# Relative-position attention: a doubled row written by ScalarE, one block copied by GpSimd, and values copied one unit later

## The chip, the cores and the metric

The kernel runs on one NeuronCore of a Trainium2 chip. The metric is the device time of one execution, in microseconds. Engines are named as in the profile: PE (TensorE, with its weight loads as PEld), DVE (VectorE), ACT (ScalarE), POOL (GpSimd) and SP (SyncE, which here issues the DMAs; its queue is SPq).

## The reference

Four layers are applied to x of 4 sequences with 1024 positions and 128 features, in float32: `x = x + attn(LN(x)) * silu(ffn(LN(x)))`, each layer with its own attn and ffn. Layers 0 to 2 (a state-space layer, an entmax attention, a recurrent layer, and their ffns) are not touched. The last layer, cut to what matters here:

```
q, k, v = split_head(x @ Wq.T), split_head(x @ Wk.T), split_head(x @ Wv.T)   # 16 heads of 8
ex = rel_embed[arange(1024) + (256 - 1024)] per head     # a table of 256 rows
srel = srel_skew(einsum('bhnd,hmd->bhnm', q, ex))        # pad by one column, reshape, cut
qk = (einsum('bhnd,bhmd->bhnm', q, k) + srel) / sqrt(8)
out = softmax(qk - 1e9 * upper_triangle) @ v  @ Wp.T + bp
ffn = down(silu(gate(x)) * up(x))                        # int8 weights, scaled by 1/127
```

So a score has a second part, the product of a query with the embedding of its distance to the key. `srel_skew` pads the products with distances by a zero column and reads them with a row length one shorter: row r of the skewed matrix begins one element further than row r - 1. The table has 256 rows and the index runs from -768 to 255: the last 256 distances take rows 0 to 255, the 256 before them the same rows again (negative indices count from the end), and all further ones row 0. The kernel subtracts row 0 from the table, which softmax does not see, so that a tile of queries needs products only for the key tiles 0 to 4 back: the block 3 back equals the block 1 back, the blocks 2 and 4 back are made from the products of the block 0 back by masks.

## The kernel before

`tile_kernel` loads the constants, runs layers 0 to 2, and then `layer3`. A tile framework gives out buffers of rotating pools, inserts the semaphores, and sets the order of instructions on each engine from the order of the program with some reordering; SP, ACT, POOL and DVE then work through their queues in that order.

In `layer3` four heads lie together in one group (partitions 32j to 32j + 8 hold head j), there are 16 groups (4 batches x 4), and each group has 8 query tiles of 128 positions, taken in the order ORDER3 = 7, 0, 6, 1, 5, 2, 4, 3. That makes 128 units n. A unit goes through these steps:

- `relative3` (called by `part`, seven half-pairs ahead): for two heads and two query tiles, PE multiplies q with the embeddings of the distances (L1914) into two PSUM tiles `pr` of the tag "tr", which has 3 buffers and which `ffn3`, `begin3`, `finish3` and `end3` use too. ACT copies each to SBUF `r` (L1916, a pool of 3 buffers). SP stores r to a DRAM tile `flat` of rows with 384 columns, the last 128 of which repeat the first 128 (four DMAs, L1919 and L1920).
- `shear3` (called by `ahead`, three units ahead): SP reads `flat` back to `rel` with a row step of 383 instead of 384, which does the skew. L1935 reads the blocks 1 and 0 back, L1937 the block of tile t = 0, L1941 the block 3 back where t is at least 3. POOL then makes the blocks 2 and 4 back and the causal mask with `affine_select` (L1945). Tile rel has two buffers for t > 3 and one for the others.
- `scores3`: PE multiplies q and k (L1978) into the only score buffer, four PSUM banks for four heads. DVE scales them, adds rel, and keeps the minimum of the negated scores (L1986 for columns without rel, L1993 with it). ACT takes the exponential and the sums (L2000).
- One tile later DVE transposes the weights (L1737), and PE multiplies them with the values (`weigh3`, L2014). The values lie in one tile `vb`, spread out by four POOL copies of `vr` (`values3`, L1899) when the last weighing of a group is through.
- `project3` loads the next group's q and k, with a POOL memset of q's first column (L1881). `finish3` (L2025 to L2035) divides by the sums, `end3` (L2041 to L2055) projects, and `begin3` and `ffn3` (L1855 to L1872: ACT's silu and copy of up, POOL's product h, PE's po) do the layer norm, q, k, v of the next batch and the ffn beside the units of chosen groups. L228 is a helper that updates x, on POOL.

Of the kernel before, what the change touches and what calls it, by code (L numbers as in the profile page):

```python
# [19 lines left out]
P = 128  # L20
# [9 lines left out]
def _constants():  # L30
    i = np.arange(P)
    row, col = i[:, None], i[None, :]
    parts = []

    def rows(a):
        a = np.asarray(a, np.float32)
        return np.ascontiguousarray(np.broadcast_to(a.reshape(1, -1), (P, a.size)))

    parts.append(("ident", np.eye(P)))
    parts.append(("tri", row <= col))  # L40
    parts.append(("neg_ssd", np.where(col >= row, 0.0, -1e30)))
    parts.append(("tril", col < row))
    parts.append(("bd8", np.kron(np.eye(16), np.ones((8, 8)))))
    parts.append(("bd16", np.kron(np.eye(8), np.full((16, 16), 1.0 / 16.0))))
    parts.append(("ones", np.ones((P, P))))

    parts.append(("sel3", (row // 32 == col // 8 % 4) & (row // 8 % 4 == col // 32)))
    parts.append(("of_a", (row // 8 % 4) == np.arange(4)[None, :]))
    parts.append(("of_t", (row % 8) == np.arange(8)[None, :]))
# [43 lines left out]
class Kit:  # L93


    def __init__(self, tc, const, const_sb):
        self.tc, self.nc = tc, tc.nc
        self.const_sb = const_sb
        self.n_copy = 0
        self.ident = self.c("ident")  # L100
        self.ident16 = const.tile([P, P], BF16, tag="ident16", name="ident16")
        self.nc.vector.tensor_copy(self.ident16, self.ident)
        self.pick = const.tile([24, 8, P], BF16, tag="pick", name="pick")

    def c(self, name):
        at, n = CONST_AT[name]
        return self.const_sb[:, at : at + n]

    def copy(self, out, in_):

# [1561 lines left out]
def layer3(k, W, x3, out, eps5, ps):  # L1672
# [12 lines left out]
    with ExitStack() as st:  # L1685
# [7 lines left out]
        def part(h):  # L1693

            at, h = divmod(h, 8)
            if at < 4 * NB:
                pair = ORDER3[h // 4 * 4 + h // 2 % 2] // 2
                if h % 2 == 0:
                    flats[at, pair] = dram.tile([2, 4, P, 384], F32, tag="flat", name="flat")
                relative3(k, W, temp, ps, flats[at, pair], group[at]["q"], at % 4, pair, h % 2)  # L1700

        def ahead(n):
# [5 lines left out]
            for n, (b, i, t) in enumerate(units):  # L1708
                yield from scores3(k, p1, p2, ps, group[n // 8], rels.pop(n), t)

        batch[0] = {}
        drain(begin3(k, W, p1, p2, temp, ps, dram, x3, 0, eps5, batch[0]))
        group[0] = {}
        drain(project3(k, p2, batch[0], 0, group[0]))
# [6 lines left out]
        weights, transposes, weighs, out_of = {}, [], [], {}  # L1721

        def transpose(n, heads):

# [14 lines left out]
                weighs.append((big, weigh(n)))  # L1739

        def weigh(n):
            nonlocal values
            b, i, t = units[n]
            at, pair = n // 8, t // 2
            if n % 8 == 2:
                out_of[at] = ps.tile([P, 8, 32], F32, tag="o", name="po")
            o = out_of[at]
            yield from weigh3(k, weights.pop((at, pair)), vb, o, pair)
            if n % 8 == 7:
                drain(values)  # L1750
                if i == 0:
                    batch[b]["on"] = p1.tile([P, 4, 256], F32, tag="on", name="on")
                finish3(k, p1, ps, o, group[at]["sums"], batch[b]["on"][:, i, :])
                if i == 3:
                    end3(k, W, temp, ps, x3, b, batch[b], out[b])
            yield
# [12 lines left out]
        for x, (n, first) in enumerate(tiles + [(len(units), 0)] * 4):  # L1769
            next(fill, None)  # L1770
            if transposes and transposes[0][0] < x:
                transpose(*transposes.pop(0)[1:])
            step()
            next(fill, None)
            last = n < len(units) and (x + 1 == len(tiles) or tiles[x + 1][0] > n)
            if not last:
                continue
            b, i, t = units[n]
            at, pos = n // 8, n % 8
            transposes += [(x, n, heads) for heads in (((0, 1), (2, 3)) if t > 3 else ((0, 1, 2, 3),))]  # L1780
            if pos == 0 and at + 1 < 4 * NB:
                group[at + 1] = {}
                project = project3(k, p2, batch[(at + 1) // 4], (at + 1) % 4, group[at + 1])
            if pos == 0 and i == 1:
                beside = ffn3(k, W, p1, temp, ps, batch[b])
            if pos == 3 and i == 2 and b + 1 < NB:
                batch[b + 1] = {}
                beside = begin3(k, W, p1, p2, temp, ps, dram, x3, b + 1, eps5, batch[b + 1])
            if pos == 0:

                next(project, None)
            part(n + 7)
            if pos == 2:
                next(project, None)
            if pos == 6 and at + 1 < 4 * NB:
                values = values3(k, p1, batch[(at + 1) // 4], vb, (at + 1) % 4)
                next(values)
            next(beside, None)
            ahead(n + 3)
        while weighs:  # L1800
            step()

# [73 lines left out]
def project3(k, p2, seq, i, group):  # L1876

    nc = k.nc
    q = p2.tile([P, 1 + T], F32, tag="q", name="q")
    kk = p2.tile([P, T], F32, tag="k", name="k")  # L1880
    nc.gpsimd.memset(q[:, 0:1], 0.0)  # L1881
# [20 lines left out]
def relative3(k, W, temp, ps, flat, q, i, pair, jp):  # L1902
# [2 lines left out]


    nc = k.nc
    r = temp.tile([P, 2, 2, 256], F32, tag="temp", name="r")
    js = (2 * jp, 2 * jp + 1)
    pr = [ps.tile([P, 2, 256], F32, tag="tr", name="pr") for _ in js]  # L1910
    for m in range(2):
# [1 line left out]
            at, t = slice(32 * j, 32 * j + 8), 2 * pair + m  # L1913
            nc.tensor.matmul(to[:, m, :], q[at, t * P : (t + 1) * P], W["emb"][at, i, :], start=True, stop=True)  # L1914
    for n, to in enumerate(pr):
        nc.scalar.copy(r[:, n], to)  # L1916
    rows = flat.rearrange("m j p u -> p j m u")
    for m in range(2):
        nc.sync.dma_start(out=rows[:, 2 * jp : 2 * jp + 2, m, 0:256], in_=r[:, :, m])  # L1919
        nc.sync.dma_start(out=rows[:, 2 * jp : 2 * jp + 2, m, 256:384], in_=r[:, :, m, 0:P])  # L1920


def shear3(k, pool, flat, t):
# [6 lines left out]
    rel = pool.tile([P, 4, min(t, 4) + 1, P], F32, tag="relb" if t > 3 else f"rels", name="rel")  # L1930
    slot = lambda back: min(t, 4) - back

    shear = lambda n: bass.AP(base.tensor, base.offset + t % 2 * 4 * P * 384 + P, [(383, P), (P * 384, 4), (1, n)])
    if t:
        nc.sync.dma_start(out=rel[:, :, slot(1) : slot(1) + 2, :].rearrange("p n s c -> p n (s c)"), in_=shear(256))  # L1935
    else:
        nc.sync.dma_start(  # L1937
            out=rel[:, :, 0, :], in_=bass.AP(base.tensor, base.offset + 2 * P, [(383, P), (P * 384, 4), (1, P)])
        )
    if t >= 3:  # L1940
        nc.sync.dma_start(out=rel[:, :, slot(3), :], in_=shear(P))  # L1941

    def select(back, sign, op, fill):

# [129 lines left out]
def tile_kernel(ctx: ExitStack, tc: tile.TileContext, I, out):  # L2074

    nc = tc.nc
    const = ctx.enter_context(tc.tile_pool(name="const", bufs=1))
    n_const = CONST_AT["pick"][0]
    const_sb = const.tile([P, n_const], F32, tag="const_sb", name="const_sb")
    nc.sync.dma_start(out=const_sb, in_=I["const"][:, 0:n_const])  # L2080
    k = Kit(tc, const, const_sb)
    eps5 = const.tile([P, 1], F32, tag="eps5", name="eps5")
    nc.vector.memset(eps5, 1e-5)
    store = ctx.enter_context(tc.tile_pool(name="x3", bufs=1, space=DRAM))
    x3 = store.tile([P, NB * NT, D], F32, tag="x3", name="x3")
    whole = ExitStack()
    xp = whole.enter_context(tc.tile_pool(name="x", bufs=1, side="right"))
    x_all = xp.tile([P, NB * NT, D], F32, tag="x_all", name="x_all")

    right = ExitStack()  # L2090
# [54 lines left out]
```

## Time and profile before

| | |
|---|---|
| median of 3 runs | 3262.25 us (3260.37 to 3266.85) |
| the profiled execution | 3261.59 us, of which its span is 3259.9 us |
| mean granted TensorE clock | 0.734 |
| PE busy over the span | 2317.2 us (71%) |
| DVE busy | 2307.1 us (71%) |
| ACT busy | 1487.5 us (46%) |
| POOL busy | 1174.5 us (36%) |
| `layer3` | about 2182 to 3260 us of the span |

Busy time of an engine is the time of its instructions without its waiting; its share is an average over four very different layers, so that the stretch of `layer3` has to be read by itself. In a list of waits, a row names the engine, its tile and line, what released it, and then the idle microseconds, how many times, and the longest. A row of groups gives busy time and mean nanoseconds of one, then the idle time just before its instructions with what ended it.

### The profile page before, as it was taken

How to read it: one execution, taken by the hardware profiler on the slowest of the kernel's cores; microseconds unless marked ns; L12 is line 12 of the kernel's file. 1: busy time of each engine (PE TensorE's matmuls, PEld its weight loads, DVE VectorE, ACT ScalarE, POOL GpSimd, SP SyncE). 2: the span in 40 equal slices, each digit the busy share in tenths (PEclk: the TensorE clock that was granted, in tenths of full speed). 3: DMA queues.
4: the chain of work that ended last, by engine and by line, in shares of the span. 5: the costliest groups of instructions: out<-in, count | busy, mean ns of one | idle time of the engine just before them, and what ended most of it. 6: DMA issues, size and time to landing. Idle time of an engine off the chain costs nothing. (4 is left out here: it accounts for less than half of the span.)

```text
span 3259.9 us, 50636 instructions
## 1 busy us (share of the span) xinstructions
PE 2317.2 (71%) x18321; PEld 1327.2 (41%) x18321; DVE 2307.1 (71%) x5534; ACT 1487.5 (46%) x3248; POOL 1174.5 (36%) x1104
## 2 busy tenths in 40 slices
PE   5787777677776777965533772557888888888885
PEld 2555555222322323651101222344545555555553
DVE  5555545878878886657868878437678778777786
ACT  4555453433333334344322561125665665755663
POOL 3344334144444444224577222332322322323322
PEclk9888888678788888985555666566766766756676
DMA  3000000100000000320433444347677677766772
GB/s 89 3 1 1 1 1 1 35 0 0 0 0 1 0 0 33 105 84 0 111 95 105 109 108 99 110 119 209 187 213 207 181 209 217 202 195 193 200 231 71
DMA packets 396446, 303.46 MB, mean 93 GB/s; under 512 B 96272, under 2 KB 380812, under 8 KB 390564
## 3 DMA queue, kind: packets, MB, share of 16 engines
q1 hardware_dynamic: 395044, 296.03, 32.2%
q10 hardware_dynamic: 1152, 4.19, 0.4%
q8 instruction: 144, 2.36, 0.3%
q14 instruction: 106, 0.87, 0.1%
HBM read 160.63 MB, written 138.94 MB: 92 GB/s over the span
## 5 line engine op out<-in xcount | busy, mean ns | idle before, releaser
L2000 ACT ACTIVATE neg<-neg,low 128x640 f32<-128x640 f32 (+7 forms) x512 | 390.0, 763 | 153.9 <-DVE low L1993 153.8
L1945 POOL TENSOR_SCALAR_AFFINE_SELECT rel<-rel 128x512 f32<-128x512 f32 x288 | 179.9, 637 | 565.6 <-DMA rel<-flat 357.3
L1737 DVE STREAM_TRANSPOSE wT<-neg 128x640 f32<-128x640 f32 (+7 forms) x512 | 362.0, 753 | 7.6 <-ACT neg L2000 6.9
L1978 PE MATMUL score<-k,q 8*128 8x512 f32 (+3 forms) x1536 | 295.0, 747 | 91.2 <-DVE low L1993 91.0
L1993 DVE CUSTOM_DVE_ANT_0 neg<-score,rel,low 128x128 f32<-128x128 f32 (+3 forms) x448 | 217.5, 516 | 152.5 <-PE score L1978 105.6
L1914 PE MATMUL pr<-emb,q 8*128 8x256 f32 x1024 | 245.2, 569 | 45.0 <-ACT r L1916 27.2
L2014 PEld LDWEIGHTS po<-wT,vb 128*32 128x32 f32 x10240 | 208.1, 140 | 143.3 <-issue 78.0
L2014 PE MATMUL po<-wT,vb 128*32 128x64 f32 (+1 forms) x10240 | 242.9, 259 | 31.7 <-issue 17.3
L1914 PEld LDWEIGHTS pr<-emb,q 8*128 8x128 f32 x1024 | 153.6, 269 | 124.4 <-ACT r L1916 62.9
L1916 ACT COPY r<-pr 128x512 f32<-128x512 f32 x256 | 138.4, 581 | 144.2 <-PE pr L1914 95.1
L1993 DVE CUSTOM_DVE_ANT_0 neg<-score,rel 128x512 f32<-128x512 f32 (+3 forms) x320 | 149.3, 520 | 26.7 <-issue 15.4
L1978 PEld LDWEIGHTS score<-k,q 8*128 8x128 f32 x1536 | 103.0, 249 | 153.9 <-DVE low L1993 127.8
L835 PE MATMUL pg<-xnT,w 128*128 128x512 f32 x256 | 148.4, 663 | 7.7 <-DVE h L839 4.5
L214 PE MATMUL pt<-ident,three 128*24 128x128 bf16 x64 | 9.2, 295 | 201.9 <-DVE three L211 201.9
L788 POOL TENSOR_TENSOR prod<-rest,kv 128x2048 f32<-128x2048 f32 x32 | 145.6, 4599 | 18.4 <-ACT rest L778 18.4
L837 PE MATMUL pu<-xin,w 128*128 128x512 f32 x256 | 140.5, 632 | 14.3 <-DVE h L839 7.9
L826 PE MATMUL po<-h,w 128*128 128x512 f32 x256 | 129.6, 627 | 27.1 <-DVE h L839 27.1
L838 ACT ACTIVATE h<-pg 128x512 f32<-128x512 f32 x128 | 75.9, 595 | 156.2 <-PE pg L835 152.7
L1986 DVE TENSOR_SCALAR_CACHE_REDUCE neg<-score 128x384 f32<-128x384 f32 (+2 forms) x192 | 79.7, 415 | 69.3 <-PE score L1978 69.3
L1050 PE MATMUL ph<-xin,upT 128*128 128x512 bf16 (+1 forms) x128 | 71.3, 588 | 78.5 <-DVE xin L1044 77.7
L1455 PE MATMUL read<-kt,const_sb 128*128 128x128 f32 x256 | 50.1, 366 | 94.2 <-POOL kt L1450 94.2
L431 PE MATMUL px<-hT,xbcT 128*128 128x512 f32 x256 | 115.4, 595 | 0.0
(621 smaller groups left out, 5690.5 us busy)
## 6 DMA issues: line engine op xcount, KB each, us to landing
flat<-r SPq DMA_DIRECT2D x256, 256.0 KB
rel<-flat SPq DMA_DIRECT2D x112, 512.0 KB
flat<-r SPq DMA_DIRECT2D x256, 128.0 KB
rel<-flat SPq DMA_DIRECT2D x96, 256.0 KB
kt<-kd SPq DMA_DIRECT2D x16, 512.0 KB
qt<-qd SPq DMA_DIRECT2D x16, 512.0 KB
kdc<-kdd SPq DMA_DIRECT2D x16, 512.0 KB
ktc<-ktd SPq DMA_DIRECT2D x16, 512.0 KB
```

What stands on the lines that cost most here:

```text
L788: nc.gpsimd.tensor_tensor(prod, attn.rearrange("p (t h g) -> p t h g", t=4, g=16)[:, t].unsqueeze(2).to_broadcast(each), kv[:, t, 1, :].re ...
L826: nc.tensor.matmul(po, W["w2"][:, e, c, :], h[:, c, :], start=(e == 0 and c == 0), stop=(e == 7 and c == 1))
L835: nc.tensor.matmul(pg, W["w1"][:, e, c * P : (c + 1) * P], xnT, start=True, stop=True)
L837: nc.tensor.matmul(pu, W["w3"][:, e, c * P : (c + 1) * P], xin, start=True, stop=True)
L1737: nc.vector.transpose(weights[at, pair][j][:, t % 2, 0 : (t + 1) * P], S[j][:, 0 : (t + 1) * P])
L1914: nc.tensor.matmul(to[:, m, :], q[at, t * P : (t + 1) * P], W["emb"][at, i, :], start=True, stop=True)
L1916: nc.scalar.copy(r[:, n], to)
L1945: nc.gpsimd.affine_select(out=rel[:, :, slot(back), :], in_=rel[:, :, slot(0), :], compare_op=op, fill=fill, base=0, pattern=[[0, 4], [-si ...
L1978: nc.tensor.matmul(sc[:, j, 0 : last - first], q[at(j), 1 + t * P : 1 + n], kk[at(j), first:last], start=True, stop=True)
L1993: nc.vector.tensor_tensor_reduce(out=neg[:, begin:last], in0=sc[:, j, begin - first : last - first], in1=rel[:, j, slot : slot + (last - b ...
L2000: nc.scalar.activation(neg[:, 0:n], neg[:, 0:n], AF.Exp, bias=here, scale=-1.0, accum_out=group["sums"][:, j, t : t + 1])
L2014: nc.tensor.matmul(o[32 * j : 32 * j + 32, 2 * pair + m.start : 2 * pair + 2, :], vb[:, kb, j].rearrange("p a d -> p (a d)"), weights[j][: ...
```

## The change

ACT copies each PSUM tile twice, 256 columns and then the first 128 of them again to columns 256 to 384, so that r is the whole doubled row. `flat` is laid out by partition, so that one DMA stores r of one `relative3` (128 rows of 6 KB). The skewed reads use a row step of 3071, and the block 3 back is copied on POOL from the block 1 back, in place of a DMA. The four POOL copies of the values are put on a list and done after the next `ahead`, or at the latest ahead of the next group's first weighing, and `ahead` comes before the step of the ffn or of the next batch. The two q tiles are made once, with their zero columns. To make room, the constants are split: those that the last layer uses stay, in a tile of their own, and the rest lies in a pool that is freed before `layer3`.

The diff, cut to its core:

```diff
+    parts.append(("sel3", (row // 32 == col // 8 % 4) & (row // 8 % 4 == col // 32)))
+    parts.append(("of_a", (row // 8 % 4) == np.arange(4)[None, :]))
+    parts.append(("of_t", (row % 8) == np.arange(8)[None, :]))
     parts.append(("tri", row <= col))
...
     def c(self, name):
         at, n = CONST_AT[name]
-        return self.const_sb[:, at : at + n]
+        n_last = CONST_AT["tri"][0]
+        return self.last_sb[:, at : at + n] if at < n_last else self.const_sb[:, at - n_last : at - n_last + n]
...
-                    flats[at, pair] = dram.tile([2, 4, P, 384], F32, tag="flat", name="flat")
+                    flats[at, pair] = dram.tile([P, 4, 2, 384], F32, tag="flat", name="flat")
...
-        batch[0] = {}
+        qs = [p1.tile([P, 1 + T], F32, tag=f"q{n}", name="q") for n in range(2)]
+        for q in qs:
+            nc.gpsimd.memset(q[:, 0:1], 0.0)
+        batch[0] = {"qs": qs}
...
+        def fill_values():
+            while ripe:
+                drain(ripe.pop())
...
             if n % 8 == 2:
+                fill_values()
                 out_of[at] = ps.tile([P, 8, 32], F32, tag="o", name="po")
...
             if n % 8 == 7:
-                drain(values)
+                ripe.append(values)
...
+            ahead(n + 3)
+            fill_values()
             next(beside, None)
-            ahead(n + 3)
...
-    q = p2.tile([P, 1 + T], F32, tag="q", name="q")
+    q = seq["qs"][i % 2]
     kk = p2.tile([P, T], F32, tag="k", name="k")
-    nc.gpsimd.memset(q[:, 0:1], 0.0)
...
-    r = temp.tile([P, 2, 2, 256], F32, tag="temp", name="r")
+    r = temp.tile([P, 2, 2, 384], F32, tag="temp", name="r")
...
     for n, to in enumerate(pr):
-        nc.scalar.copy(r[:, n], to)
-    rows = flat.rearrange("m j p u -> p j m u")
-    for m in range(2):
-        nc.sync.dma_start(out=rows[:, 2 * jp : 2 * jp + 2, m, 0:256], in_=r[:, :, m])
-        nc.sync.dma_start(out=rows[:, 2 * jp : 2 * jp + 2, m, 256:384], in_=r[:, :, m, 0:P])
+        nc.scalar.copy(r[:, n, :, 0:256], to)
+        nc.scalar.copy(r[:, n, :, 256:384], to[:, :, 0:P])
+    nc.sync.dma_start(out=flat[:, 2 * jp : 2 * jp + 2], in_=r)
...
-    shear = lambda n: bass.AP(base.tensor, base.offset + t % 2 * 4 * P * 384 + P, [(383, P), (P * 384, 4), (1, n)])
+    shear = lambda n: bass.AP(base.tensor, base.offset + t % 2 * 384 + P, [(3071, P), (768, 4), (1, n)])
...
     if t >= 3:
-        nc.sync.dma_start(out=rel[:, :, slot(3), :], in_=shear(P))
+        nc.gpsimd.tensor_copy(rel[:, :, slot(3), :], rel[:, :, slot(1), :])
...
-    const_sb = const.tile([P, n_const], F32, tag="const_sb", name="const_sb")
-    nc.sync.dma_start(out=const_sb, in_=I["const"][:, 0:n_const])
-    k = Kit(tc, const, const_sb)
+    last_sb = const.tile([P, n_last], F32, tag="last_sb", name="last_sb")
+    nc.sync.dma_start(out=last_sb, in_=I["const"][:, 0:n_last])
+    const_sb = xp.tile([P, n_const - n_last], F32, tag="const_sb", name="const_sb")
+    nc.sync.dma_start(out=const_sb, in_=I["const"][:, n_last:n_const])
+    k = Kit(tc, xp, const_sb, last_sb)
```

In the built program, the last layer has 256 more ACT copies, 80 more POOL copies, 14 POOL memsets fewer and 384 store DMAs and 80 read DMAs fewer; ACT has 171 activation-table loads instead of 169 over the whole kernel. PE and DVE have as many instructions as before, with small changes of order in the last layer. The order in layers 0 to 2 is the same.

More of the change, by code (lines that the diff above doesn't have):

```diff
@@ L45, in _constants @@
     parts.append(("ones", np.ones((P, P))))
-    parts.append(("sel3", (row // 32 == col // 8 % 4) & (row // 8 % 4 == col // 32)))
-    parts.append(("of_a", (row // 8 % 4) == np.arange(4)[None, :]))
-    parts.append(("of_t", (row % 8) == np.arange(8)[None, :]))
     parts.append(("sel16", (row // 16) == np.arange(8)[None, :]))
@@ L93, with __init__ @@
 class Kit:
-    def __init__(self, tc, const, const_sb):
+    def __init__(self, tc, const, const_sb, last_sb):
         self.tc, self.nc = tc, tc.nc
-        self.const_sb = const_sb
+        self.const_sb, self.last_sb = const_sb, last_sb
         self.n_copy = 0
@@ L1720, in layer3 @@
         beside, project, values = iter(()), iter(()), iter(())
-        weights, transposes, weighs, out_of = {}, [], [], {}
+        weights, transposes, weighs, out_of, ripe = {}, [], [], {}, []
+        def fill_values():
+            while ripe:
+                drain(ripe.pop())
         def transpose(n, heads):
@@ L1741, in weigh @@
         def weigh(n):
-            nonlocal values
             b, i, t = units[n]
@@ L1786, in layer3 @@
             if pos == 3 and i == 2 and b + 1 < NB:
-                batch[b + 1] = {}
+                batch[b + 1] = {"qs": qs}
                 beside = begin3(k, W, p1, p2, temp, ps, dram, x3, b + 1, eps5, batch[b + 1])
@@ L1937, in shear3 @@
         nc.sync.dma_start(
-            out=rel[:, :, 0, :], in_=bass.AP(base.tensor, base.offset + 2 * P, [(383, P), (P * 384, 4), (1, P)])
+            out=rel[:, :, 0, :], in_=bass.AP(base.tensor, base.offset + 2 * P, [(3071, P), (768, 4), (1, P)])
         )
     if t >= 3:
-        nc.sync.dma_start(out=rel[:, :, slot(3), :], in_=shear(P))
+        nc.gpsimd.tensor_copy(rel[:, :, slot(3), :], rel[:, :, slot(1), :])
     def select(back, sign, op, fill):
@@ L2077, in tile_kernel @@
     const = ctx.enter_context(tc.tile_pool(name="const", bufs=1))
-    n_const = CONST_AT["pick"][0]
-    const_sb = const.tile([P, n_const], F32, tag="const_sb", name="const_sb")
-    nc.sync.dma_start(out=const_sb, in_=I["const"][:, 0:n_const])
-    k = Kit(tc, const, const_sb)
+    whole = ExitStack()
+    xp = whole.enter_context(tc.tile_pool(name="x", bufs=1, side="right"))
+    n_last, n_const = CONST_AT["tri"][0], CONST_AT["pick"][0]
+    last_sb = const.tile([P, n_last], F32, tag="last_sb", name="last_sb")
[3 more added lines that the diff above has]
+    k = Kit(tc, xp, const_sb, last_sb)
     eps5 = const.tile([P, 1], F32, tag="eps5", name="eps5")
@@ L2085, in tile_kernel @@
     x3 = store.tile([P, NB * NT, D], F32, tag="x3", name="x3")
-    whole = ExitStack()
-    xp = whole.enter_context(tc.tile_pool(name="x", bufs=1, side="right"))
     x_all = xp.tile([P, NB * NT, D], F32, tag="x_all", name="x_all")
```

## The prediction

> **What bounds the kernel now.** Only the last layer's code changes (and where some constants lie), so I first cut the span where that layer's loop begins and ends, at 2180 and 3260 us, with the start of its loop by itself.
>
> ```profile
> core 0: us, PE busy (x) PEld busy (x) DVE busy (x) ACT busy (x) POOL busy (x), PEclk, DMA share, GB/s
> 2180.00:2210.00 30.00, 17.93 (x72) 13.15 (x72) 1.84 (x9) 10.46 (x18) 6.59 (x8) 0.54 1.08 295
> 2210.00:3240.00 1030.00, 866.59 (x13274) 545.63 (x13275) 806.48 (x2547) 625.71 (x1474) 288.53 (x412) 0.68 0.68 195
> ```
>
> In the 1030 us of the main stretch PE is busy 84%, DVE 78%, ACT 61%, POOL 28%, the DMA engines 68%. No engine is full; PE and DVE come nearest, so what counts is who waits for whom. Next, the waits of 2220 to 3240 us (engine, line, what it waited for: us, times, longest):
>
> ```profile
> POOL rel L1945 <- DMA rel<-flat: 341.5, 71, 13.8
> ACT neg L2000 <- DVE low L1993: 143.3, 67, 7.8
> DVE neg L1993 <- PE score L1978: 111.3, 59, 9.7
> ACT r L1916 <- PE pr L1914: 89.3, 53, 5.7
> PE score L1978 <- DVE low L1993: 78.1, 82, 5.4
> POOL vb L1899 <- PE po L2014: 76.3, 14, 12.0
> PEld pr L1914 <- ACT r L1916: 59.6, 44, 5.1
> POOL q L1881 <- PE score L1978: 49.4, 10, 7.8
> ```
>
> DVE waits for PE's next scores and PE for DVE to empty the one score buffer: these two pass the work to and fro, and PE's other products (pr, po) lie between. The longest wait, POOL's for the read-back rel, counts only if somebody waits for POOL. Tile rel answers that for 2215 to 3260 us ("who waited for it"):
>
> ```profile
>   POOL rel L1945: 341.5, 71
>   POOL h L1867: 1.9, 1
>   ACT r L1916: 0.3, 1
> ```
>
> DVE, the only reader of the finished rel, is not in the list. Set side by side unit by unit in the rows, a rel's last select ends at least 2.4 us (5 in 100: 4.4; median 11.5) before DVE takes it, in every unit but the first. So the way out to DRAM and back, which the change lightens most, is early by 2.4 us or more. What ACT does is nearer the path: PE's pr products wait for ACT's copies out of PSUM (59.6 us at the weight loads, 27.0 at the products), since three "tr" PSUM buffers are all there are.
>
> **ACT's second copy (added, the largest term).** Each of 256 PSUM tiles now needs a 128x2x256 copy and a 128x2x128 copy.
>
> ```profile
> L1916 ACT COPY r<-pr 128x512 f32<-128x512 f32 x240 | 129.5, 581 | 130.4 <-PE pr L1914 89.3 <-POOL x L228 16.0 <-issue 14.5
> L1866 ACT COPY up<-pgu 128x256 f32<-128x256 f32 x48 | 16.9, 375 | 0.0
> ```
>
> The second row is the new copy's shape: 0.375 us alone, 0.28 to 0.32 from start to start in a run of copies (a pair of 512-wide ones takes 1.07, so 0.53 each, against 0.581 alone). I take 0.32: 256 x 0.32 = 82 us (bounds 72 and 96), which lifts ACT in the stretch from 61% to about 68%. That is no bound by itself; it costs where PE waits for the copy's end. Counted row by row: 35 times PE starts on a pr, pgu or similar "tr" tile within 0.05 us of the end of an r copy, and 28 of these are followed by DVE waiting for the scores queued behind on PE. One of them:
>
> ```profile
> 2875.18 1.07 ACT L1916 COPY r<-pr 128x512 f32<-128x512 f32 x2 [1.70 <-issue]
> 2875.82 2.07 PE L1914 MATMUL pr<-emb,q 8*128 8x256 f32 x8 [0.65 <-ACT r L1916]
> ...
> 2878.07 1.66 PE L1978 MATMUL score<-k,q 8*128 8x384 f32 x8 [0.17 <-DVE low L1993]
> ...
> 2879.80 0.62 DVE L1993 CUSTOM_DVE_ANT_0 neg<-score,rel,low 128x384 f32<-128x384 f32 x1 [1.79 <-PE score L1978]
> ```
>
> Such a release comes later by its own tile's second copy (0.32) or by that and what has piled up before it (up to 0.86): 28 x 0.32 = 9, 28 x 0.86 = 24; with 0.54, between them, 15 us. Exps pushed back by the copies are the other way onto DVE: shifting ACT's rows by 0.32 after each r copy, as far as idle time does not take it up, moves 92 of 512 exps and delays DVE's transposes in 10 units, 6 us in all. They are the same stretches as above for the most part, so I add nothing and keep 6 for the upper bound. The instruction order also holds two more activation-table loads (1.28 us each in the rows): 0 to 2.6, taken 1, since about half of ACT's time has slack.
>
> **One store instead of four (removed), and reads 12 KB apart.** SP issues 128 stores for 512; four take about 2 us of SP (0.36 to 0.51 each), one about 0.5. Bytes and the pieces' destinations stay, so the DMA engines gain little from it; they gain by the third read, 80 x 256 KB in 512-byte packets (28 ns each by the rows), some 61,000 of them, about 107 us of 16 engines' 1030. All of it ends in rel's lead of 2.4 us and more: 0 in the main stretch. At the start it does not, since 28 stores go out before the first read:
>
> ```profile
> 2203.16 0.51 SPq L1935 DMA_DIRECT2D rel<-flat  x1
> 2207.42 2.52 POOL L1945 TENSOR_SCALAR_AFFINE_SELECT rel<-rel 128x512 f32<-128x512 f32 x4 [15.52 <-DMA rel<-flat]
> 2208.69 0.35 DVE L1993 CUSTOM_DVE_ANT_0 neg<-score,rel,low 128x128 f32<-128x128 f32 x1 [13.91 <-POOL rel L1945]
> ```
>
> DVE waits 13.9 us there. ACT's 14 copies, which feed the stores, lose 5.6 us of waiting for store buffers but gain 14 x 0.32 = 4.5 us of work, and the last store is issued with the last copy, at about 2202; the select waits for one read less but for a copy. Gain 0 to 5, taken 3.
>
> [...]
>
> **The third block by GpSimd (added).** 80 copies of 128x512. Rows of POOL copies: 128 elements a partition take 0.25 to 0.30 us (L1639, L1646), 1024 take 1.03 (L1899); the select over the same block takes 0.637. I take 0.55 (0.3 to 1.03): 44 us, POOL from 28% to 32%, and each rel ready 0.55 later, inside the 2.4. Cost 0; if that cover were gone, 80 x 0.55 = 44. POOL's h of the ffn (48 x 0.73) stands behind these copies, and PE waits for h 16 us today; one copy ahead of each ffn step would be at most a few us.
>
> Whether a POOL copy stops DVE is not shown, for before has no POOL copy of a whole block beside DVE. The nearest row says no: POOL's selects take 635/637/644 ns (least, median, most) whatever DVE does.
>
> [...]
>
> **Values, q and constants (moved).** POOL's copies of vb wait 76.3 us for the old group's last weigh and its memset of q 49.4 us, with rel's selects queued behind. Later values and 14 memsets fewer free these selects, which again are early; the new place puts the vb copies ahead of the first weigh of the next group, and PE has no wait for vb in the list. 0, with 5 either way for the changed order of parts and reads. The constants' second load is at the very start, under other loads: 0. Layers 0 to 2 keep their order.
>
> **Sum.** The profiled execution took 3261.59 us (1.7 above its span, 0.66 below the median of the runs). 3261.6 + 15 + 1 - 3 = 3274.6, on the scale of the median 3275. Bounds: 9 + 0 - 5 - 5 = -1 to 24 + 6 + 2.6 + 5 = +38.
>
> **Rivals.** (1) Faster: SP and the DMA engines are nearer the path than rel's lead says. PE waits 18 us for POOL's h (16.0 at the weight loads, 2.4 at the products) and ACT 16 us for POOL's x (L228); were POOL late in these because of the reads and head-of-line waits, half of 34 would come back, 17, with 5 at the start, against half of the ACT term, 8: about -14, 3248. It decides if these two waits fall by half. Against: h is mostly late by ACT's up (46.9). (2) No change: ACT's 39% of idle time takes the copies, as where ACT waited for PE (89.3); 28 releases cost under 0.2 each, 5, and the start gives 3: 3264. (3) Much slower: reading at a row step of 12 KB, or the copies on POOL, makes rel late. From a loss of 4.4 us of lead on, 5 units in 100 stall; if half the 128 units wait 0.5 us, +32, with the ACT term 3308.
>
> **How the numbers follow.** ACT's copies on the path 0.43; rel late 0.10; no change 0.17; faster 0.30. A measurement of this kernel can tell about 0.2% (6.5 us) from no change. Likeliest 3275, by itself 3269 to 3290; the range 3244 to 3300 reaches over the faster case and part of the slow one.
>
> **What would show it.** Right: ACT busier by about 80 us in the stretch, PE's waits for ACT r up by 10 to 30, DVE's for score by about as much, POOL's waits for DMA rel down, and still no DVE wait for rel. Wrong: PE's waits for r unchanged (2), h and x waits halved (1), DVE waiting for POOL rel after the first unit (3), or POOL copies and DVE rows that lengthen each other.

## The result and the profile after

The changed kernel takes 3286.32 us (median of 7 runs, 3275.9 to 3305.63) against 3264.28 (7 runs, 3258.98 to 3267.68) for the kernel before on the same chip: ratio 1.0073 with a 95% interval of 1.0046 to 1.0100, slower by 0.73%, or 22 us by the medians. The forecast was 3275. The profiled execution took 3278.0 us (span 3276.2, clock 0.736), 16.4 us more than that of before.

First the main stretch again. Columns as before: PE, weight loads, DVE, ACT, POOL, then granted clock and DMA share.

```profile
2210.00:3240.00 1030.00, 868.54 (x12946) 550.86 (x12950) 791.33 (x2511) 686.28 (x1699) 328.88 (x474) 0.68 0.56 174
```

ACT and POOL have the added work, the DMA engines are relieved (0.68 to 0.56), and DVE does 15 us less in the same 1030 us, because the work has slid back. Now the waits (engine, tile, line, what it waited for: us, times, longest), with those that the forecast rested on:

```profile
POOL rel L1949 <- DMA rel<-flat: 352.2, 60, 12.3
DVE neg L2001 <- PE score L1986: 121.1, 61, 12.0
...
PEld pr L1924 <- ACT r L1927: 57.5, 41, 5.7
DVE neg L2001 <- issue: 44.7, 10, 11.4
...
PE pr L1924 <- ACT r L1927: 25.8, 16, 4.2
...
DVE wT L1747 <- ACT neg L2008: 13.4, 23, 1.3
```

PE's waits for ACT's r ahead of pr did not rise: 59.6 became 57.5 and 27.0 became 25.8. With those ahead of pgu, pv and pp (26.2 before, 31.1 after) they are 1.6 us longer in all. That is the term that made most of the forecast, and it is not there. DVE's waits for scores in the columns with rel did rise, by 9.8 (from 111.3), with 4.5 more put down to "issue" (from 40.2); in the columns without rel they fell by 5.9 (44.1 to 38.2). Together they rose by 8.4, so something else on PE comes late. Who waited for tile rel:

```profile
  POOL rel L1949: 352.2, 60
  POOL rel L1953: 84.7, 30
  DVE neg L2001: 3.5, 1
```

rel stayed early, as forecast: DVE waited once. And the groups of ACT's two copies and POOL's third block (busy us, mean ns, idle before):

```profile
L1926 ACT COPY r<-pr 128x512 f32<-128x512 f32 x240 | 140.5, 586 | 100.3 <-PE pr L1924 76.4 <-POOL x L230 12.2 <-ACT r L1927 5.9
L1927 ACT COPY r<-pr 128x256 f32<-128x256 f32 x240 | 91.3, 381 | 0.0
L1949 POOL COPY rel<-rel 128x512 f32<-128x512 f32 x78 | 47.5, 609 | 461.9 <-DMA rel<-flat 352.2 <-DVE low L2001 90.5 <-DVE wT L1747 18.9
```

The copies out of PSUM now find 30 us less idle time before them (100.3, before 130.4): ACT took that part of the new work out of waiting.

**Where the time is lost.** I measured each group from its first DVE product to the next group's (the last one to DVE's first s behind it). The four groups that run the ffn beside their units (the second of each batch, i = 1) take 303.5 us instead of 284.0; the other twelve take 763.4 instead of 766.3. So the loop's whole loss lies in four groups, and most of it (16 of 19.5 us) in one place each: at the fifth unit (tile t = 5) DVE takes the first score tile and then waits for the second, while PE works on the ffn. Windows over exactly these four waits, before:

```profile
2309.77:2319.49 9.72, 9.47 (x46) 6.67 (x48) 0.01 (x2) 3.65 (x10) 2.18 (x3) 0.70 0.25 81
2572.43:2579.10 6.67, 6.30 (x44) 4.47 (x44) 0.01 (x3) 3.58 (x10) 2.18 (x3) 1.00 0.46 135
2828.80:2834.14 5.34, 4.97 (x37) 3.50 (x39) 0.01 (x1) 2.65 (x9) 2.17 (x3) 1.00 0.60 172
3094.60:3101.30 6.70, 6.33 (x44) 4.47 (x44) 0.01 (x3) 3.58 (x10) 2.17 (x3) 1.00 0.48 137
```

and after:

```profile
2306.92:2318.91 11.99, 11.66 (x60) 8.28 (x63) 0.01 (x2) 4.58 (x13) 2.62 (x4) 0.82 0.17 67
2570.77:2582.20 11.43, 10.97 (x61) 8.18 (x64) 0.02 (x3) 4.68 (x13) 2.17 (x3) 0.71 0.17 69
2840.44:2851.85 11.41, 10.96 (x60) 8.16 (x63) 0.01 (x2) 4.67 (x13) 2.17 (x3) 0.71 0.17 70
3107.44:3117.16 9.72, 9.37 (x51) 6.70 (x55) 0.01 (x1) 4.62 (x13) 2.17 (x3) 0.70 0.20 82
```

Four waits of 28.4 us together became 44.6, which is +16 us, about what this profiled execution lost. DVE is empty, PE is over 93% busy, ACT is less than half busy, and the granted clock (the column after POOL) is full in three of four before and in none after. What PE does there is shown by its timeline in the second batch (start, us, line, operation, count); before:

```profile
2568.76 2.93 PE L1871 MATMUL po<-downT,h 128*128 128x128 f32 x12
2571.61 1.13 PE L1914 MATMUL pr<-emb,q 8*128 8x256 f32 x8
```

and after:

```profile
2567.09 0.80 PE L1882 MATMUL po<-downT,h 128*128 128x128 f32 x2
2567.82 1.22 PE L1924 MATMUL pr<-emb,q 8*128 8x256 f32 x2
2568.97 0.80 PE L1882 MATMUL po<-downT,h 128*128 128x128 f32 x2
2569.69 1.22 PE L1924 MATMUL pr<-emb,q 8*128 8x256 f32 x2
2570.84 2.08 PE L1882 MATMUL po<-downT,h 128*128 128x128 f32 x8
2572.84 1.22 PE L1924 MATMUL pr<-emb,q 8*128 8x256 f32 x4
```

The same 12 products of the ffn's third step and 8 products pr of the next half-pair, in another order: 12, 8 became 2, 2, 2, 2, 8, 4. Nothing in the change asks for that. The framework that sets the order of instructions chose it, and (as one_act_copy shows below) it goes back to 12, 8 when ACT's second copies, two for each half-pair, are taken out. In both traces DVE falls idle 3.7 us after PE turns from the scores to this block; DVE gets its scores 10.3 us after the turn before (2568.76 to 2579.10) and 15.1 after (2567.09 to 2582.20).

The clock stretches it. In the traces of before and after it is granted at 0.50 or 1.00 alone, in stretches of whole multiples of 3.41 us. Before, windows on these steps:

```profile
2564.81:2568.22 3.41, 3.41 (x7) 1.52 (x6) 0.00 (x0) 1.64 (x6) 2.05 (x3) 0.50 0.75 200
2568.22:2571.64 3.42, 3.42 (x15) 2.66 (x14) 2.67 (x13) 0.00 (x0) 1.32 (x3) 0.50 0.00 0
2571.64:2575.05 3.41, 3.41 (x20) 2.76 (x20) 0.77 (x4) 2.39 (x7) 0.48 (x1) 1.00 0.06 23
```

and after:

```profile
2560.34:2563.75 3.41, 3.38 (x12) 1.92 (x7) 2.19 (x5) 3.38 (x9) 2.33 (x4) 0.50 0.80 262
2563.75:2567.16 3.41, 3.41 (x7) 1.17 (x5) 0.00 (x0) 1.48 (x6) 2.64 (x4) 0.50 0.32 126
2567.16:2570.58 3.42, 3.42 (x9) 1.93 (x8) 3.24 (x15) 0.00 (x0) 0.71 (x2) 0.50 0.00 0
2570.58:2573.99 3.41, 3.41 (x13) 2.29 (x12) 0.20 (x2) 0.38 (x1) 0.00 (x0) 0.50 0.00 0
2573.99:2577.40 3.41, 3.41 (x10) 2.77 (x9) 0.00 (x0) 2.27 (x6) 0.56 (x1) 0.50 0.24 99
2577.40:2580.82 3.42, 2.96 (x18) 2.19 (x18) 0.00 (x0) 1.29 (x4) 1.61 (x3) 1.00 0.33 131
```

Before, 2.9 us of the block run at half rate, after 10.3. The 12 products take 2.9 us here, at half rate, and 1.5 us in the third batch of before, at full rate. Counting a microsecond at half rate as half a microsecond of work, the block is 8.9 us of work before (2.9 / 2 + 7.5) and 9.9 after (10.3 / 2 + 4.8): 1 us for the changed order itself, and the other 3.7 for the clock. This is an estimate worked out from these rows for one batch, not measured by itself.

### The profile page after: what moved, and what is told of

Read it like the earlier page. It is cut to its first block, busy times and chain, and to the rows that moved or that the text cites. A ratio compares the mean times of both kernels' runs of the same rounds, so it can differ in the third digit from the quotient of the medians.

```text
span 3276.2 us, 50451 instructions
## 1 busy us (share of the span) xinstructions
PE 2332.3 (71%) x18319; PEld 1341.2 (41%) x18321; DVE 2307.3 (70%) x5534; ACT 1557.9 (48%) x3506; POOL 1216.8 (37%) x1170
## 5 line engine op out<-in xcount | busy, mean ns | idle before, releaser
L1747 DVE STREAM_TRANSPOSE wT<-neg 128x640 f32<-128x640 f32 (+7 forms) x512 | 361.6, 754 | 14.6 <-ACT neg L2008 13.4
L1924 PE MATMUL pr<-emb,q 8*128 8x256 f32 x1024 | 259.2, 568 | 51.8 <-ACT r L1927 25.8
L2022 PE MATMUL po<-wT,vb 128*32 128x64 f32 (+1 forms) x10240 | 236.2, 255 | 40.0 <-issue 23.4
L1949 POOL COPY rel<-rel 128x512 f32<-128x512 f32 x80 | 48.7, 609 | 477.3 <-DMA rel<-flat 352.2
L1924 PEld LDWEIGHTS pr<-emb,q 8*128 8x128 f32 x1024 | 165.8, 268 | 130.9 <-ACT r L1927 60.8
L1926 ACT COPY r<-pr 128x512 f32<-128x512 f32 x256 | 150.1, 586 | 110.1 <-PE pr L1924 83.8
L2001 DVE CUSTOM_DVE_ANT_0 neg<-score,rel 128x512 f32<-128x512 f32 (+3 forms) x320 | 149.2, 521 | 25.1 <-issue 9.3
L790 POOL TENSOR_TENSOR prod<-rest,kv 128x2048 f32<-128x2048 f32 x32 | 145.2, 4571 | 18.4 <-ACT rest L780 18.4
L1457 PE MATMUL read<-kt,last_sb 128*128 128x128 f32 x256 | 49.4, 363 | 94.2 <-POOL kt L1452 94.2
```

What stands on the lines that cost most here:

```text
L790: nc.gpsimd.tensor_tensor(prod, attn.rearrange("p (t h g) -> p t h g", t=4, g=16)[:, t].unsqueeze(2).to_broadcast(each), kv[:, t, 1, :].re ...
L1747: nc.vector.transpose(weights[at, pair][j][:, t % 2, 0 : (t + 1) * P], S[j][:, 0 : (t + 1) * P])
L1926: nc.scalar.copy(r[:, n, :, 0:256], to)
L2001: nc.vector.tensor_tensor_reduce(out=neg[:, begin:last], in0=sc[:, j, begin - first : last - first], in1=rel[:, j, slot : slot + (last - b ...
L2022: nc.tensor.matmul(o[32 * j : 32 * j + 32, 2 * pair + m.start : 2 * pair + 2, :], vb[:, kb, j].rearrange("p a d -> p (a d)"), weights[j][: ...
```

## The experiments

Theory A when these began: ACT's second copies are the loss, either because they hold a PSUM buffer longer (A1, the forecast's own mechanism) or in another way (A2). Later runs split A2 into the changed order on PE at the ffn's third step (A2a) and the copies as work on a path (A2b). Rivals: the moved values, reads and ffn steps (B); POOL's copy and the reads 12 KB apart (C). Each ratio is against the kernel before on the same chip, with its 95% interval.

**one_act_copy**: the second copy goes; two stores write the doubled columns.

```diff
-        nc.scalar.copy(r[:, n, :, 256:384], to[:, :, 0:P])
-    nc.sync.dma_start(out=flat[:, 2 * jp : 2 * jp + 2], in_=r)
+    nc.sync.dma_start(out=flat[:, 2 * jp : 2 * jp + 2, :, 0:256], in_=r[:, :, :, 0:256])
+    nc.sync.dma_start(out=flat[:, 2 * jp : 2 * jp + 2, :, 256:384], in_=r[:, :, :, 0:P])
```

> The changed kernel, but ACT copies each PSUM tile once (256 columns) and SP stores the row in two DMAs (256 columns, and the first 128 again), as the kernel before did; the rest of the change stays. Theory A (ACT's second copies are the cost): the loss of 22 us against the kernel before goes, to 0 or a gain of up to 5 us, ratio 0.998 to 1.001, and the four groups with the ffn (i = 1) take about 71 us each again instead of 76. Theory B (the moved order of reads, ffn steps and values is the cost): stays near 1.007. Theory C (GpSimd's copies and the reads 12 KB apart are the cost): stays near 1.007.

Measured 1.0016 [0.9996, 1.0036]. Most of the loss is gone, and PE's order at the third step is 12, 8 again. The four waits:

```profile
2308.81:2314.16 5.35, 4.98 (x37) 3.52 (x39) 0.02 (x3) 2.66 (x9) 2.17 (x3) 1.00 0.45 147
2574.45:2581.43 6.98, 6.62 (x54) 4.70 (x54) 0.01 (x2) 3.67 (x10) 2.17 (x3) 1.00 0.36 116
2837.92:2847.73 9.81, 9.57 (x54) 6.77 (x56) 0.02 (x3) 3.74 (x10) 2.17 (x3) 0.70 0.25 80
3100.80:3106.23 5.43, 5.07 (x45) 3.59 (x46) 0.01 (x2) 2.75 (x9) 2.18 (x3) 1.00 0.43 145
```

27.6 us in all, as before the change, and the ffn's groups take 289.1 us. The copies are the cause; how is still open. PE's waits for ACT's r are 63.3 and 31.1 here, longer than with the second copies, which speaks against A1.

**copy_from_sbuf**: the second copy reads r, so that the PSUM tile is free after the first.

```diff
-        nc.scalar.copy(r[:, n, :, 256:384], to[:, :, 0:P])
+        nc.scalar.copy(r[:, n, :, 256:384], r[:, n, :, 0:P])
```

> The changed kernel, but ACT's second copy reads the SBUF row it has just written instead of the PSUM tile: the same number of ACT instructions of the same size, but PE gets the PSUM buffer back one copy earlier. Theory A1 (the second copies cost because they hold the three PSUM buffers): PE's waits for ACT r fall to the level of before and most of the 22 us goes, ratio about 1.002. Theory A2 (they cost as work on ACT, ahead of the exps and of the ffn's silu, or by the order that the scheduler gives PE, which is the same here as in the changed kernel): stays at 1.005 to 1.009.

Measured 1.0073 [1.0048, 1.0099], no gain over the changed kernel. PE's waits for ACT's r are 55.8 and 25.1, like 57.5 and 25.8 with the copy out of PSUM. That a tile is held longer by its own second copy is not what costs. (The copy out of a half-pair's second tile still stands behind the first tile's second copy here.)

**third_by_dma**: the third block is read by a DMA again.

```diff
-        nc.gpsimd.tensor_copy(rel[:, :, slot(3), :], rel[:, :, slot(1), :])
+        nc.sync.dma_start(out=rel[:, :, slot(3), :], in_=shear(P))
```

> The changed kernel, but the block 3 back is read by a DMA of its own again (80 reads of 256 KB), with the new row step; no POOL copies. Theory A: stays at 1.005 to 1.009, since nothing waits for rel. Theory C (POOL's copies block DVE, or make rel and the ffn's h late): ratio 1.001 or less.

Measured 1.0119 [1.0093, 1.0144], slower than the changed kernel, which neither theory expected. The ffn's groups are alike (304.9 us); the other twelve take 783.6 instead of 763.4. In this layout the kernel with POOL's copy is the faster one.

**old_order**: values and ffn steps in their old places.

```diff
-                ripe.append(values)
+                drain(values)
...
+            next(beside, None)
             ahead(n + 3)
             fill_values()
-            next(beside, None)
```

> The changed kernel with the place of the next ffn step ahead of the reads, and with the values copied directly after the group's last weighing, both as before. Theory A: stays at 1.005 to 1.009. Theory B: ratio 1.001 or less.

Measured 1.0071 [1.0049, 1.0094], as the changed kernel: the moved steps neither cost nor bring anything that can be seen, and PE's mixed order at the third step stays.

**ffn_down_together**: the changed kernel with PE's order pinned, so that the next half-pair's pr and the weighings come behind the third step's last product. The other engines keep their order.

```diff
-            step()
+            u = units[n] if n < len(units) else (0, 0, 0)
+            with tc.issue_after(batch[u[0]]["down"]) if u[1] == 1 and n % 8 in (3, 4) else ExitStack():
+                step()
...
-            part(n + 7)
+            with tc.issue_after(batch[b]["down"]) if i == 1 and pos == 3 else ExitStack():
+                part(n + 7)
...
-                    nc.tensor.matmul(po[:, a, :], h[:, c, a * P : (a + 1) * P], W["downT"][:, c, :], start=(c == 0), stop=(c == 2))
+                    seq["down"] = nc.tensor.matmul(po[:, a, :], h[:, c, a * P : (a + 1) * P], W["downT"][:, c, :], start=(c == 0), stop=(c == 2)).ins
```

> The changed kernel, with issue-order edges on PE alone: in the four groups with the ffn, the six products po of the ffn's third step stand together again, ahead of the four products pr of the next half-pair, as in the kernel before; in the changed kernel they stand po, pr, po, pr, 4 po, 2 pr. ACT, POOL, DVE and SP have the same instructions in the same order as the changed kernel, ACT's second copies included. Theory A2a (ACT's second copies cost only through the order that the scheduler gives PE there): the 16 us go, ratio 1.000 to 1.003, and DVE's wait ahead of the second score tile of position 4 falls from 11 us to about 6.5. Theory A2b (they cost as work on ACT): stays at 1.005 to 1.009.

Measured 1.0031 [1.0017, 1.0045]: with all of ACT's copies in place, 0.42 points (14 us) of the 0.73 are back. The wait fell to 7.3 us in one batch only; in the other three the clock stayed at half for part of it, as here in the third and fourth:

```profile
2837.69:2847.43 9.74, 9.54 (x53) 6.69 (x55) 0.01 (x1) 4.29 (x12) 2.17 (x3) 0.71 0.20 82
3103.84:3113.62 9.78, 9.55 (x53) 6.73 (x55) 0.01 (x1) 4.29 (x12) 2.17 (x3) 0.70 0.20 81
```

The profile does not show where the 14 us come back: the four waits are 39.4 us there, 5 less than after the change, and the ffn's groups take 303.6 us, no less than 303.5. A profile is one execution, here of 3275.6 us against a median of 3273, and after the change of 3278.0 against 3286. So this gain rests on the run times alone, and their intervals leave 4 to 24 us for it. The 0.31% that remain are not told apart from the 0.16% of one_act_copy.

**one_copy_mixed**: the reverse. In one_act_copy, PE alone is given the mixed order 2, 2, 2, 2, 8, 4 at the same four places, by dependencies between its own instructions.

```diff
-            nc.tensor.matmul(to[:, m, :], q[at, t * P : (t + 1) * P], W["emb"][at, i, :], start=True, stop=True)
+            x = nc.tensor.matmul(to[:, m, :], q[at, t * P : (t + 1) * P], W["emb"][at, i, :], start=True, stop=True).ins
+            if seq:
+                k.tc.add_manual_dep(x, seq["down"].name, mybir.DependencyInfo(mybir.DependencyClass.NoSync, mybir.DependencyReason.DATA))
+                if m == 0:
+                    seq["after"] = x
+                    next(beside)
...
+                    m = nc.tensor.matmul(po[:, a, :], h[:, c, a * P : (a + 1) * P], W["downT"][:, c, :], start=(c == 0), stop=(c == 2)).ins
+                    if "after" in seq:
+                        k.tc.add_manual_dep(m, seq["after"].name, mybir.DependencyInfo(mybir.DependencyClass.NoSync, mybir.DependencyReason.DATA))
```

> The reverse of that: one_act_copy (a single ACT copy, two stores) with edges that give PE the mixed order po, pr, po, pr, 4 po, 2 pr at these four places; nothing else differs from one_act_copy on any engine. Theory A2a: slower than one_act_copy by 12 to 18 us, ratio to the kernel before 1.005 to 1.008, with DVE's wait there at 10 to 12 us. Theory A2b: as one_act_copy, 1.000 to 1.003.

Measured 1.0052 [1.0032, 1.0072]: 0.36 points (12 us, by the intervals 3 to 21) over one_act_copy, with nothing but 20 products in another order in four groups. The profile shows it there: the ffn's groups take 302.9 us instead of 289.1. The four waits:

```profile
2312.52:2323.55 11.03, 10.58 (x53) 7.85 (x56) 0.01 (x1) 4.02 (x11) 2.17 (x3) 0.72 0.22 71
2579.83:2589.68 9.85, 9.39 (x55) 6.67 (x57) 0.01 (x2) 4.11 (x11) 2.17 (x3) 0.75 0.25 82
2840.92:2852.37 11.45, 11.00 (x60) 8.17 (x63) 0.01 (x1) 4.12 (x11) 2.17 (x3) 0.71 0.21 69
3107.52:3118.80 11.28, 10.82 (x61) 8.04 (x64) 0.01 (x2) 4.12 (x11) 2.17 (x3) 0.72 0.21 70
```

43.6 us, as after the change (44.6), against 27.6 without it. Taken out and put in, the order on PE moves 12 to 14 us: A2a carries the larger part.

**doubled_by_pool**: GpSimd makes the doubled columns, ACT copies once.

```diff
-        nc.scalar.copy(r[:, n, :, 256:384], to[:, :, 0:P])
+    nc.gpsimd.tensor_copy(r[:, :, :, 256:384], r[:, :, :, 0:P])
```

> The changed kernel with the doubled columns copied by GpSimd from SBUF (one 128x512 copy for each relative3, 128 in all) instead of by ACT; one store of 6 KB rows. PE has the order of one_act_copy. Theory A2a and A2b alike: 0.998 to 1.002, since ACT is relieved and PE's order is the old one. [...]

Measured 1.0064 [1.0049, 1.0079], outside the 0.998 to 1.002 of both theories. The four waits are back to 31.0 us (order 12, 8), but the other twelve groups take 780.9. POOL copies r in its queue order, behind work on rel that waits for a read, and ACT waits 17.6 us for POOL's work on tile rel, where it waited 0.3 in the kernel before. That these waits are the loss in the twelve groups is not shown.

**before_third_by_pool**: the kernel before, with POOL's copy of the third block as its only change.

```diff
-        nc.sync.dma_start(out=rel[:, :, slot(3), :], in_=shear(P))
+        nc.gpsimd.tensor_copy(rel[:, :, slot(3), :], rel[:, :, slot(1), :])
```

> The kernel before with one part of the change alone: the block 3 back copied by GpSimd from the block 1 back instead of read by a DMA. My prediction's step (rel is early, so nothing follows): 0.998 to 1.002. If the change's POOL copy gains 15 us, as the difference between the changed kernel and third_by_dma would have it: 0.994 to 0.997. PE's order at the ffn's third step is 2 po, pr, 4 po, 3 pr here in three of the four groups; by theory A2a that may cost up to 8 us.

Measured 0.9994 [0.9979, 1.0009]: no difference, as forecast for that part. The milder mixing on PE (4, 2, 8, 6 products in three groups) cost nothing that can be seen; in these three groups the wait was 6.1, 6.1 and 10.6 us.

**ffn_spread_before** and **ffn_spread_after**: can the ffn's stall be avoided? The ffn in eight half steps, each placed behind a unit's scores, once in before_third_by_pool and once in the changed kernel (22 more table loads than before).

```diff
+            if n < len(units) and units[n][1] == 1:
+                with tc.issue_after(k.score):
+                    next(beside, None)
...
-            next(beside, None)
+            if i != 1:
+                next(beside, None)
...
+            yield
             po = ps.tile([P, 2, D], F32, tag="tr", name="po")
```

> The kernel before with the block 3 back by GpSimd (before_third_by_pool) and the ffn of the four groups cut into eight half steps (three pgu pairs, or six po), each placed behind the scores of the next tile by an issue-order edge, so that no long row of ffn products stands ahead of scores that DVE waits for. ACT has 22 more activation-table loads (1.28 us each). If the loss found so far sits in scores queued behind the ffn's products at half clock, this gains: DVE waits some 15 to 16 us per such group in the kernel before, 60 us in all; if half of that goes and the table loads take back a third of it, 15 to 20 us, ratio 0.993 to 0.996. If PE has as much to do at half clock anyway, or the table loads hold the exps, 1.000 to 1.005.

> The changed kernel with the same eight half steps. PE's order in the four groups is now the same as in ffn_spread_before, so that the difference to it is what the rest of the change costs with no difference of order there: ACT's second copies as work, the 6 KB rows, the late values. By theory A2a alone: as ffn_spread_before within 5 us. If ACT's copies cost as work as well (DVE's transposes behind later exps, 6 us in my prediction): 5 to 12 us slower than it.

Measured 1.0079 [1.0061, 1.0097] and 1.0145 [1.0122, 1.0168], both outside what was expected of them. In the first, the wait at the fifth unit shrank to 21.2 us in all, but one of 10.6 to 12.5 us arose in each batch two units later. In the second, the wait at the fifth unit is 13.6 us in all, and the later one 12.7 to 14.2 in each batch. The profile puts this later wait down to ACT's copies in ffn_spread_after, and to "issue" in ffn_spread_before. These rows have it and DVE's wait for the exps, of ffn_spread_before:

```profile
DVE neg L1998 <- issue: 78.5, 19, 12.5
DVE wT L1737 <- ACT neg L2005: 20.0, 34, 1.7
```

and of ffn_spread_after:

```profile
DVE neg L2006 <- ACT r L1932: 53.6, 4, 14.2
DVE wT L1747 <- ACT neg L2013: 33.7, 36, 2.5
```

PE's order in the ffn's groups is all but the same in both, and there the kernel with ACT's copies takes 313.5 us instead of 306.7. This fits A2b, the copies as work (some 7 us here), but does not show it: the 6 KB rows and the late values differ too. The other twelve groups take 788.7 us instead of 778.1, and there PE's order differs as well, so the 0.66 points (22 us) between the two kernels are not split into work and order. In the changed kernel itself DVE waits 13.4 us for the exps.

**third_by_pool_together**: before_third_by_pool, with the third step kept together on PE by the same edges as in ffn_down_together (placed at pos 2 and 3).

> before_third_by_pool, with issue-order edges on PE that keep the six products po of the ffn's third step together in all four groups (there they stand 2 po, pr, 4 po, 3 pr in three of the four); all other engines have the same order. If the mixed order costs where it is half as mixed as in the changed kernel: 3 to 8 us faster than before_third_by_pool, 0.997 to 0.999, the fastest so far. If a single pr between them costs nothing: 0.998 to 1.001.

Measured 0.9987 [0.9972, 1.0002], with full clock in all four waits (24.6 us). The lowest ratio of all, but not shown to be faster than the kernel before or than before_third_by_pool.

**one_copy_third_by_dma**: one_act_copy with the third block read by DMA, the edits of one_act_copy and third_by_dma together.

> one_act_copy with the block 3 back read by a DMA again, at the new row step of 12 KB. third_by_dma was about 15 us slower than the changed kernel; is it the read? If reading the third block at this row step, or the longer DMA work, is what costs: ratio 1.004 to 1.008. If it was a matter of the order and of ACT's second copies beside it: 1.000 to 1.003, as one_act_copy.

Measured 1.0108 [1.0087, 1.0129]: 0.92 points (30 us) over one_act_copy. As in third_by_dma, the replaced read costs in the new layout and not in the old. DVE waits 5.1 us for rel, once, so the read isn't seen to come late for it; the extra time stands in DVE's waits for scores (138.5 and 47.7, against 115.9 and 41.4; 27.3 against 37.0 are put down to "issue"), and PE's order differs from one_act_copy's in several groups. PE's waits for POOL's h of the ffn are twice as long, 40.5 us against 20.1 (27.9 in third_by_dma against 18.4 after the change): POOL makes h in the same queue as the selects that wait for the reads. Whether the reads at a row step of 12 KB cost by themselves, by way of h or by the order that comes with them was not told apart.

## Why the prediction was right or wrong

**Direction and range: right, the mechanism wrong.** Slower was the likeliest case; +22 us (0.73%) was measured where +13 us (0.4%) was forecast, and 3286 lies within 3244 to 3300.

**ACT's copies as a wait of PE: wrong.** This is the step that failed: "28 x 0.32 = 9, 28 x 0.86 = 24; with 0.54, between them, 15 us". PE's waits for r rose by 1.6 us in all, where 10 to 30 were forecast. copy_from_sbuf, which takes a tile's second copy off its release, gains nothing, and one_act_copy, without second copies, has the longer waits ahead of pr. The releases found in before do not add up as delays: in the rows PE, after a wait, starts within 0.07 us of an r copy's end 35 times before the change and 27 times after. ACT waited less for pr (89.3 to 76.4) and took a part of the copies from idle time. That the 15 us are near the truth is luck. What the runs showed in its place is that ACT's copies changed the order of PE's instructions at the ffn's third step: 14 us come back when it is pinned, 12 us are lost when it is imposed. The forecast looked at the built order for table loads and for "small changes of order", and did not price those on PE, though they stood there before any run.

**ACT's work: too high.** Forecast 82 us (72 to 96); busy time rose from 1487.5 to 1557.9, by 70, just under the lower bound.

**Exps pushed back: not shown either way.** 6 us were worked out and left out as "the same stretches". DVE's wait for the exps rose from 6.9 to 13.4, but it is 11.0 in one_act_copy and 10.2 in one_copy_mixed, which have no second copies. So some 2 to 3 us of the rise go with the copies, and the rest is there without them. Why the clock stays at half in three of the four waits of ffn_down_together was not taken apart.

**The start: 3 forecast, 0.3 measured.** The first read is issued 2.8 us sooner, yet DVE starts only 0.25 sooner:

```profile
2200.36 0.41 SPq L1943 DMA_DIRECT2D rel<-flat  x1
...
2206.61 0.61 POOL L1949 COPY rel<-rel 128x512 f32<-128x512 f32 x1 [15.45 <-issue]
2207.18 2.39 POOL L1953 TENSOR_SCALAR_AFFINE_SELECT rel<-rel 128x512 f32<-128x512 f32 x4
2208.44 0.35 DVE L2001 CUSTOM_DVE_ANT_0 neg<-score,rel,low 128x128 f32<-128x128 f32 x1 [13.54 <-POOL rel L1953]
```

POOL, which waited for the read by the forecast's row of before, now starts with its copy 0.8 us sooner (2207.42 to 2206.61) and reaches the selects 0.24 sooner.

**Stores and reads off the path: right.** The DMA share fell by 0.12, and no gain is to be seen. In third_by_dma, which keeps the third read, it is 0.62 in the same 1030 us: the rest of the change took off as much as the read, not the "little" of the forecast. The 61,000 packets of the third read were a wrong sum: 80 reads of 256 KB in 512-byte packets are 40,960, at 28 ns some 72 us of 16 engines and not 107. before_third_by_pool, which drops these reads alone, has 354,206 packets on its page where before has 396,446. Nothing in the forecast's sum rested on it. **POOL's third block: right**, 0.609 us each where 0.55 was taken, one DVE wait of 3.5 us, and no difference in before_third_by_pool. **Values and order: right** (old_order); the q tiles were not tested by themselves. The two table loads were not measured by themselves.

**POOL's copies beside DVE: no lengthening.** The forecast left open whether a POOL copy stops DVE. After the change POOL's 80 copies of the third block take 608 to 612 ns, whether one of DVE's products with rel runs beside them (40) or not. DVE's products of 512 columns that read scores and rel alone take 682 ns in the mean beside such a copy (46) and 679 otherwise (82); over all of them it is 680 ns before the change and 680 after. Those of 384 columns take 550 ns (14) and 549 (50).

**The rivals.** Faster was to come from halved waits for h and x: x went from 16.0 to 12.2, h at the weight loads from 16.0 to 14.7. No change was to come from ACT's idle time taking the copies up, and on PE's waits for r that rival was right; it fell by the order. A late rel did not come.

## What to carry to other kernels

Where a framework orders the instructions, an edit on one engine is also an edit of the others' order: compare the built orders of the busiest engine in every stage, and price each difference at the places where another engine already waits. When the cause is in dispute, pin the order and leave the work, then leave the order and take the work; here both moved 12 to 14 us. Read such a gain from many run times: the single profile of the pinned kernel did not show it. And a wait that grew by more than any added instruction lasts is a reason to look at the granted clock in just that window.

## What the runs showed of the hardware

The four waits form two groups by clock. Where the granted clock was 1.00 throughout they lasted 5.3 to 7.3 us, where it was lower 9.6 to 15.2, in every kernel but the two with the ffn spread out. In the profiles of the five kernels with the mixed order 2, 2, 2, 2, 8, 4 (the changed one, copy_from_sbuf, third_by_dma, old_order, one_copy_mixed) it was low in 20 of 20 waits; in five with 12, 8 (before, one_act_copy, ffn_down_together, doubled_by_pool, third_by_pool_together) in 7 of 20. With the order 4, 2, 8, 6 (three groups each of before_third_by_pool and one_copy_third_by_dma) it was low in 4 of 6. So the order goes with the clock but does not settle it alone.

In the traces of before and after the granted clock is 0.50 or 1.00 in every record (182 stretches before, 196 after), and each stretch but the last lasts a whole multiple of 3.41 us. One such window of busy PE did not bring the full clock: from 2560.34 to 2577.40 us after the change, five windows in a row show PE busy 3.38 to 3.42 us at 0.50, before the sixth has 1.00. In both fences the window just before the full clock has more weight-load time (2.66 and 2.77 us) than those ahead of it; whether this brings the full clock was not tested.
